# Reordering VectorE's work inside an attention step, and redistributing a small table over other steps

## The chip, the core and the metric

The kernel runs on one core of one Trainium2 chip. The metric is the device time of one execution in microseconds (us), as the median of several runs. Beside it there is one profiled execution, taken by the hardware profiler. Its times stand in the views that this document reads. The engines are called as in the profile: PE is TensorE (PEld its weight loads), DVE is VectorE, ACT is ScalarE, POOL is GpSimd and SP is SyncE. L488 means line 488 of the kernel before.

## What is computed

The input is 32 sequences of 256 tokens with 128 features, in float32. The reference, cut to what matters here:

```python
h = layernorm(x) * (1 + ca) + sa                       # per sequence scale and shift
n = h * rsqrt(mean(h * h) + eps)
q, k, v = n @ W_qkv.T + b_qkv                          # 16 heads of 64
scores = where(causal_mask, -inf, einsum('bqhd,bkhd->bhqk', q, k))
attn = softmax(scores, axis=-2)                        # over the queries
x = x + ga * (attn @ v @ W_o.T + b_o)
h = layernorm(x) * (1 + cb) + sb
x = x + gb * moe(h)      # 32 experts in 4 groups: 2 groups and 6 experts a token,
                         # a shared expert and an anchor expert
```

The softmax runs over the queries of one key. So one partition holds one key's scores, and the sums over the queries scale the values, not the weighted sums.

## The kernel before

**Chunks and steps.** The 8192 tokens are 16 chunks of 512 tokens (2 sequences). Attention runs in steps: step s handles chunk s // 8 and two heads of it, number s % 8. There are 128 such steps and three more that drain. This document calls s % 8 the position of a step, p0 to p7. The expert stage follows after the steps.

**What one step does** (loop at L1098 to L1132). Each engine works through its own queue in the order in which the program was written, so the order of the Python calls is the order on each engine.

- `score_products(s)` (L519, PE): the scores of two sequences times two heads, into four PSUM buffers (pool `ps_sc`, four buffers).
- `lowest(s, b, h)` (L539, DVE): adds the mask, writes the scores into `e` and finds the lowest (the queries were negated, so this is the greatest). It is called four times a step, for sequence b and head h. One call is two pieces of 256 and 128 columns, each with a small read of the accumulator.
- `exponential(s, b, h)` (L549, ACT): four calls a step, each for the `e` of one `lowest`. It also yields the sums.
- `inverse_sums(s - 1)` (L557, DVE) and `scaled_values(s - 1)` (L568, POOL): the values over the sums, as `vs`.
- `weighted_sums(s - 2)` (L586, PE) and `heads_out(s - 2)` (L597, ACT, output `z`).
- `query_product(s + 2)` (L483, PE) and its eviction from PSUM (L488, DVE). `key_product(s + 2)` (L495, PE) and its eviction (L500, ACT).
- `project(s - 3)` (L607, PE) and one quarter of the next values: `values` (L469, PE) and its eviction (L476, DVE).

The query, key and value products share two PSUM buffers (pool `ps_mm`) in turn. So the value product of a step takes the buffer of that step's query product, and waits until the queries are evicted (L488). A product after that takes the buffer of the keys, and waits for their eviction (L500). Two further products use this pool: `route_logits` (L664, at p3) and `route_ranks` (L752 and L756, at p0), each put last in its step.

**Portions.** The rest of the work (the two layer norms and the routing) is cut into portions. A table (L872 to L913) gives each portion a step relative to its chunk, and a place in the step: TOP is ahead of the score products, MID is between the keys' eviction and the projection, END is behind the values. Since eight steps make a chunk, a portion has the same position in every chunk. Those that matter here:

- p0: `route_marks` (L810, DVE, at TOP and MID), `route_ranks` (END). `norm1_scale` (L449 to L452, POOL, END) follows `route_ranks` on POOL.
- p1: `route_weights` (L818 to L828, DVE, TOP), loads of x (END), `rest_bias` (L620, POOL, END).
- p2: `route_place` (L775 to L787, DVE, TOP), `norm1_moments` (L356, DVE, MID), which needs the loaded x.
- p3: `norm2_turn` and `rest_gate` (L652, L628, DVE, TOP), `route_logits` (END).
- p5: `norm1_modulate` (L383, POOL, END). p6: `route_merge` (L692 to L695, DVE, TOP) and `route_groups` (L702 to L715, DVE, MID).
- p7: `route_mask` and `route_top` (DVE), `norm2_modulate` (L383, POOL, END).

**The first tiles' table.** When the routing of chunk 6 is known (step 72), the first tiles of the expert stage can be listed. Nine portions do this with DVE instructions of 4 to 64 elements a partition: `open_first` (L1041), `count_taken` (L1046) and seven steps a to g of `first_tiles.steps()` (L975 to L1034). They depend on each other in this order. Before, they sit at END of steps 80 to 88, one a step (L1084). The table is first read when the expert stage starts, after step 130.

Of the kernel before, what the change touches and what calls it, by code (L numbers as in the profile page):

```python
# [30 lines left out]
NP = H // 2  # L31
# [14 lines left out]
EARLY = 6  # L46
# [10 lines left out]
def adaln_block_kernel(  # L57
# [80 lines left out]
    def late_loads():  # L138

        nc.sync.dma_start(out=wd_sb, in_=w_down.rearrange("(k p) m -> p k m", p=P))  # L140
        nc.sync.dma_start(out=ad_sb, in_=an_down.rearrange("(k p) m -> p k m", p=P))
        nc.sync.dma_start(out=sg_sb, in_=sh_gate)
        nc.sync.dma_start(out=su_sb, in_=sh_up)
        for h in range(P // SI):
            nc.sync.dma_start(out=sd_sb[h * SI : (h + 1) * SI], in_=sh_down)
# [68 lines left out]
    def write_blank(i):  # L214
        nc.sync.dma_start(
            out=rows_d[i * CH : (i + 1) * CH].rearrange("(p i) f -> p i f", i=NT), in_=blank
        )
# [98 lines left out]
    NS = NCH * NP  # L316
# [3 lines left out]
    with ExitStack() as actx:  # L320
# [159 lines left out]
        def query_product(s):  # L480
            c, t = divmod(s, NP)
            pq = ps_mm.tile([P, CH], F32, tag="mm", name=f"pq_{s}")
            nc.tensor.matmul(  # L483
                pq, wqkv_sb[:, 0, t * P : (t + 1) * P], chunk[c]["n"], start=True, stop=True
            )
            q = qk.tile([P, CH], F32, tag="q", name=f"q_{s}")
            step_of["q", s] = q
            return lambda: nc.vector.tensor_scalar(  # L488
                q, pq, -1.0, negbq[:, t : t + 1], ALU.mult, ALU.add
            )  # L490
# [13 lines left out]
        def score_products(s):  # L504


            q, k = step_of.pop(("q", s)), step_of.pop(("k", s))
            ps = []
            for b in range(BPC):
                o = b * S  # L510
                pb = [
                    ps_sc.tile([P, 3 * P], F32, tag="sc", name=f"psc_{s}_{b}_{h}")
                    for h in range(2)
                ]
                for kb in range(2):
                    cols = slice(0, 2 * P) if kb == 0 else slice(2 * P, 3 * P)
                    for h in range(2):
                        r = slice(h * DH, (h + 1) * DH)
                        nc.tensor.matmul(  # L519
                            pb[h][:, cols],  # L520
                            k[r, o + kb * P : o + (kb + 1) * P],
                            q[r, o + kb * P : o + S],
                            start=True,
                            stop=True,
                        )
                ps.append(pb)
            step_of["ps", s] = ps
            step_of["e", s] = [[None, None] for _ in range(BPC)]
            step_of["mn", s] = st.tile([P, BPC, 2, 2], F32, tag="mn", name=f"mn_{s}")
            step_of["sm", s] = st.tile([P, BPC, 2, 2], F32, tag="sm", name=f"sm_{s}")  # L530

        def lowest(s, b, h):

            ps, mn = step_of["ps", s][b][h], step_of["mn", s]
            e = sp.tile([P, 3 * P], F32, tag="e", name=f"e_{s}_{b}_{h}")
            step_of["e", s][b][h] = e
            for kb in range(2):
                cols = slice(0, 2 * P) if kb == 0 else slice(2 * P, 3 * P)
                nc.vector.tensor_tensor_reduce(  # L539
                    e[:, cols], ps[:, cols], mask[:, cols], 1.0, 3e38,  # L540
                    ALU.add, ALU.min, mn[:, b, kb, h : h + 1],
                )

        def exponential(s, b, h):

            e, mn, sm = step_of["e", s][b][h], step_of["mn", s], step_of["sm", s]
            for kb in range(2):
                cols = slice(0, 2 * P) if kb == 0 else slice(2 * P, 3 * P)
                nc.scalar.activation(  # L549
                    e[:, cols], e[:, cols], AF.Exp, bias=mn[:, b, kb, h : h + 1], scale=-1.0,  # L550
                    accum_out=sm[:, b, kb, h : h + 1],
                )

        def inverse_sums(s):
            sm = step_of.pop(("sm", s))
            rc = st.tile([P, BPC, 2, 2], F32, tag="rc", name=f"rc_{s}")
            nc.vector.reciprocal(  # L557
                rc.rearrange("p b k h -> p (b k h)"), sm.rearrange("p b k h -> p (b k h)")
            )
            step_of["rc", s] = rc  # L560

        def scaled_values(s):
            c, t = divmod(s, NP)
            vt, rc = step_of["v", s // HALF], step_of.pop(("rc", s))
            vs = vsp.tile([P, BPC * 2, 2, DH], F32, tag="vs", name=f"vs_{s}")
            col = (t % HALF) * P
            for b in range(BPC):
                nc.gpsimd.tensor_tensor(  # L568
                    vs[:, 2 * b : 2 * b + 2],
                    vt[:, 2 * b : 2 * b + 2, col : col + P].rearrange(  # L570
                        "p k (h d) -> p k h d", h=2
                    ),
                    rc[:, b].unsqueeze(3).to_broadcast([P, 2, 2, DH]),
                    ALU.mult,
                )
            step_of["vs", s] = vs

        def weighted_sums(s):
            vs, es = step_of.pop(("vs", s)), step_of.pop(("e", s))
            pav = ps_av.tile([P, CH], F32, tag="av", name=f"pav_{s}")  # L580
            for b in range(BPC):
                o = b * S
                for kb in range(2):
                    for h in range(2):
                        e = es[b][h]
                        nc.tensor.matmul(  # L586
                            pav[h * DH : (h + 1) * DH, o + kb * P : o + S],
                            vs[:, 2 * b + kb, h, :],
                            e[:, 0 : 2 * P] if kb == 0 else e[:, 2 * P : 3 * P],
                            start=kb == 0,  # L590
                            stop=kb == 1,
                        )
            step_of["pav", s] = pav

        def heads_out(s):
            z = zp.tile([P, CH], F32, tag="z", name=f"z_{s}")
            nc.scalar.copy(z, step_of.pop(("pav", s)))  # L597
            step_of["z", s] = z
# [138 lines left out]
        def new_counts(c):  # L737
            counts[c] = rt.tile([P, NT + 1, NG], F32, tag="cnt", name=f"cnt_{c}", bufs=2)
            return counts[c]
# [130 lines left out]
        TOP, MID, END = range(3)  # L870
# [197 lines left out]
        portions = {}  # L1068

        soon = {-6: 0, -5: 0, -4: 0, -3: 0, -2: 1, -1: 1, 0: 2, 1: 2}  # L1070
        for c in range(NCH):
            for at, where, portion in table[0 if c else NORM1 :]:
                if c == 1 and portion is load_x:
                    continue
                if c == 1:
                    at = soon.get(at + NP, at + NP) - NP
                portions.setdefault(c * NP + at, []).append((where, portion, c))

        def deal(s, where):
            for w, portion, c in portions.get(s, []):  # L1080
                if w == where:
                    portion(c)

        for n, portion in enumerate([open_first, count_taken, *first_tiles.steps()]):  # L1084
            portions.setdefault((EARLY + 4) * NP + n, []).append((END, lambda c, p=portion: p(), 0))
        nc.gpsimd.memset(new_counts(0), 0.0)
        nc.gpsimd.tensor_scalar_mul(counts[0][:, 0, :], origin, first)
        for at in range(min(portions), 0):
# [9 lines left out]
        for s in range(NS + LAG + 1):  # L1098
            if s == NP + 1:
                late_loads()  # L1100
            ahead = s + 2 < NS
            deal(s, TOP)
            if s < NS:
                score_products(s)
                for h in range(2):
                    lowest(s, 0, h)
                for h in range(2):
                    exponential(s, 0, h)
            if 1 <= s <= NS:
                inverse_sums(s - 1)  # L1110
                scaled_values(s - 1)
            if LAG <= s < NS + LAG:
                weighted_sums(s - LAG)
                heads_out(s - LAG)
            if s < NS:
                lowest(s, 1, 0)
                exponential(s, 1, 0)
            if ahead:
                query_product(s + 2)()
            if s < NS:  # L1120
                lowest(s, 1, 1)
                exponential(s, 1, 1)
            if ahead:
                key_product(s + 2)()
            deal(s, MID)
            if LAG < s <= NS + LAG:
                project(s - LAG - 1)
            if s // HALF + 1 < 2 * NCH:
                values(s // HALF + 1, s % HALF)()
            deal(s, END)  # L1130
            for i in blanks[s * 3 : s * 3 + 3]:
                write_blank(i)  # L1132
# [364 lines left out]
```

## Time and profile before

| | |
|---|---|
| runs before: median of 3 (lowest to highest) | 1473.55 us (1470.64 to 1475.26) |
| the profiled execution: its own time | 1488.63 us |
| its span, first to last instruction | 1486.9 us |
| mean granted PE clock over the span | 0.98 |
| busy, share of the span: PE, DVE, ACT, POOL | 95%, 69%, 54%, 52% |
| the attention steps | from about 27 us to about 935 us of the span |
| DVE L539 (lowest), 256 and 128 columns | 406 and 285 ns each |
| DVE L488 (queries' eviction) | 750 ns each, 128 of them |
| ACT L500 (keys' eviction) | 669 ns each |
| POOL L383 (modulate) | 732 ns each |

The page of a profile gives the busy time of each engine, the span in 40 slices, and the costliest groups of instructions with the idle time of their engine just before them and what ended it. Behind the page stand further views. The table of windows gives busy times and the granted PE clock of a stretch. The list of waits says who waited for whom. The timeline shows instructions in order of time: start, duration, engine, line, and in brackets the idle time before it and who ended that. An idle engine costs time only where the engine that sets the pace waits for it.

### The profile page before, as it was taken

The page shows a single profiled execution, that of the slowest core. Times are in us where ns is not written, and L with a number is a line of the kernel's source. Part 1 is how long each engine was busy: PE and PEld are TensorE (multiplying, and loading weights), DVE is VectorE, ACT ScalarE, POOL GpSimd, SP SyncE. Part 2 cuts the span into 40 slices and gives each one's busy share as a digit, 9 for nine tenths or more (in the row PEclk, how much of TensorE's full clock was granted, in tenths as well). Part 3 has the DMA queues.
Part 4 walks back from the last instruction along what each step waited for, and adds up shares of the span by engine and source line. Part 5 has one row for each costly group of instructions (what it writes and reads, how often), then busy time and mean ns, then how long its engine had stood idle before and what let it go on. Part 6 is the DMA issues. An engine that isn't in the chain of part 4 may idle for free. (4 is left out here: it accounts for less than half of the span.)

```text
span 1486.9 us, 29744 instructions
## 1 busy us (share of the span) xinstructions
PE 1413.1 (95%) x8559; PEld 901.8 (61%) x8559; DVE 1033.0 (69%) x4277; ACT 803.5 (54%) x2767; POOL 767.4 (52%) x1294
## 2 busy tenths in 40 slices
PE   7999999999999999999999999889999999999994
PEld 3566666666666666666666666456566666666662
DVE  5666768778777677788787677656755656766664
ACT  4777667677676677667666767323233333333331
POOL 3545457567667657567676655634332233344333
PEclk9999999999999999999999999999999999999997
DMA  4873521121121220221211210577767678887872
GB/s 145 287 241 96 201 70 37 48 68 33 54 65 36 55 57 29 67 53 33 70 43 44 54 32 28 144 191 195 185 183 187 173 210 231 240 251 234 254 201 75
DMA packets 183584, 182.26 MB, mean 123 GB/s; under 512 B 81520, under 2 KB 142656, under 8 KB 178944
## 3 DMA queue, kind: packets, MB, share of 16 engines
q1 hardware_dynamic: 172112, 159.62, 38.8%
q0 software_dynamic: 10624, 20.21, 4.1%
q8 instruction: 71, 1.16, 0.3%
q14 instruction: 89, 0.73, 0.2%
q10 hardware_dynamic: 688, 0.53, 0.1%
HBM read 121.37 MB, written 59.70 MB: 122 GB/s over the span
## 5 line engine op out<-in xcount | busy, mean ns | idle before, releaser
L549 ACT ACTIVATE e<-e,mn 128x256 f32<-128x256 f32 (+1 forms) x1024 | 453.8, 445 | 235.2 <-DVE mn L539 224.8
L539 DVE CUSTOM_DVE_ANT_0 e<-psc,mask 128x256 f32<-128x256 f32 (+1 forms) x1024 | 306.1, 346 | 31.9 <-PE psc L519 28.1
L568 POOL TENSOR_TENSOR vs<-v,rc 128x256 f32<-128x256 f32 x256 | 151.5, 613 | 248.5 <-DVE rc L557 215.9
L1273 POOL DMA_INDIRECT y_d<-y,iy x140 | 137.9, 985 | 235.0 <-ACT y L1270 202.7
L519 PEld LDWEIGHTS psc<-q,k 64*128 64x128 f32 x2048 | 172.7, 194 | 88.7 <-issue 74.3
L1240 DVE TENSOR_TENSOR a<-a,pu 128x512 f32<-128x512 f32 x175 | 120.0, 686 | 148.5 <-PE pu L1237 110.6
L519 PE MATMUL psc<-q,k 64*128 64x256 f32 (+1 forms) x2048 | 211.1, 347 | 0.0
L586 PE MATMUL pav<-e,vs 128*64 128x256 f32 (+1 forms) x2048 | 198.8, 337 | 5.9 <-POOL vs L568 5.9
L1239 ACT ACTIVATE a<-pg 128x512 f32<-128x512 f32 x175 | 104.5, 597 | 183.1 <-PE pg L1236 126.3
L1262 PEld LDWEIGHTS py<-wd_sb,a 128*128 128x128 f32 x1120 | 146.6, 192 | 75.2 <-issue 51.6
L549 ACT ACTIVATION_READ_ACCUMULATOR e<-e,mn 128x1 f32 x1024 | 192.2, 188 | 0.0
L1236 PE MATMUL pg<-h,wg 128*128 128x512 f32 x350 | 181.4, 600 | 0.0
L1237 PE MATMUL pu<-h,wu 128*128 128x512 f32 x350 | 180.1, 596 | 0.0
L607 PEld LDWEIGHTS po<-wo_sb,z 128*128 128x128 f32 x1024 | 135.0, 193 | 59.7 <-issue 56.1
L488 DVE TENSOR_SCALAR q<-pq,negbq 128x512 f32<-128x512 f32 x128 | 96.0, 750 | 103.1 <-PE pq L483 103.0
L586 PEld LDWEIGHTS pav<-e,vs 128*64 128x64 f32 x2048 | 128.9, 139 | 61.1 <-POOL vs L568 6.3
L1262 PE MATMUL py<-wd_sb,a 128*128 x1120 | 148.5, 276 | 5.4 <-DVE a L1241 5.4
L852 POOL DMA_INDIRECT rows_d<-rows,ix x128 | 130.0, 1016 | 37.2 <-issue 34.1
L483 PE MATMUL pq<-n_t,wqkv_sb 128*128 128x512 f32 x256 | 144.9, 648 | 0.7 <-ACT n_t L302 0.7
L476 DVE TENSOR_TENSOR v<-pv,bv_sb 128x512 f32<-128x512 f32 x128 | 88.2, 689 | 75.6 <-PE pv L469 75.5
L607 PE MATMUL po<-wo_sb,z 128*128 128x128 f32 x1024 | 136.3, 277 | 0.0
L469 PE MATMUL pv<-wqkv_sb,n_t 128*128 128x512 f32 x256 | 133.7, 606 | 2.2 <-DVE q L488 1.2
(231 smaller groups left out, 1835.5 us busy)
## 6 DMA issues: line engine op xcount, KB each, us to landing
bt<-cd SPq DMA_DIRECT2D x70, 512.0 KB
rows_d<-blank SPq DMA_DIRECT2D x69, 360.0 KB
rw<-rows_d SPq DMA_DIRECT2D x35, 360.0 KB
wg<-in_w_gate_dram SPq DMA_DIRECT2D x35, 256.0 KB
wu<-in_w_up_dram SPq DMA_DIRECT2D x35, 256.0 KB
bt<-cd SPq DMA_DIRECT2D x140, 64.0 KB
s<-y_d SPq DMA_DIRECT2D x32, 256.0 KB
mb<-mod_dram SPq DMA_DIRECT2D x31, 256.0 KB
```

The lines of the kernel that those rows point to most:

```text
L469: nc.tensor.matmul(pv, chunk[c]["n"][:, i * P : (i + 1) * P], wqkv_sb[:, 2, j * CH : (j + 1) * CH], start=True, stop=True,)
L483: nc.tensor.matmul(pq, wqkv_sb[:, 0, t * P : (t + 1) * P], chunk[c]["n"], start=True, stop=True)
L519: nc.tensor.matmul(pb[h][:, cols], k[r, o + kb * P : o + (kb + 1) * P], q[r, o + kb * P : o + S], start=True, stop=True,)
L539: nc.vector.tensor_tensor_reduce(e[:, cols], ps[:, cols], mask[:, cols], 1.0, 3e38, ALU.add, ALU.min, mn[:, b, kb, h : h + 1],)
L549: nc.scalar.activation(e[:, cols], e[:, cols], AF.Exp, bias=mn[:, b, kb, h : h + 1], scale=-1.0, accum_out=sm[:, b, kb, h : h + 1],)
L568: nc.gpsimd.tensor_tensor(vs[:, 2 * b : 2 * b + 2], vt[:, 2 * b : 2 * b + 2, col : col + P].rearrange("p k (h d) -> p k h d", h=2), rc[:, ...
L586: nc.tensor.matmul(pav[h * DH : (h + 1) * DH, o + kb * P : o + S], vs[:, 2 * b + kb, h, :], e[:, 0 : 2 * P] if kb == 0 else e[:, 2 * P : 3 ...
L607: nc.tensor.matmul(chunk[c]["po"][:, i, :], z[:, i * P : (i + 1) * P], wo_sb[:, t, :], start=t == 0 and i == 0, stop=t == NP - 1 and i == ...
L1236: nc.tensor.matmul(pg, t["wg"][:, k, :], t["h"], start=True, stop=True)
L1237: nc.tensor.matmul(pu, t["wu"][:, k, :], t["h"], start=True, stop=True)
L1262: nc.tensor.matmul(t["py"][:, i, :], a[:, i * P : (i + 1) * P], w, start=k == 0 and i == 0, stop=k == KU and i == NT - 1,)
L1273: sent = nc.gpsimd.indirect_dma_start(out=y_d[:, :], out_offset=bass.IndirectOffsetOnAxis(ap=ix[:, i : i + 1], axis=0), in_=y[:, i, :], in ...
```

## The change

There are two edits in the main loop and its portions.

First, in every step both remaining `lowest` calls (sequence 1, heads 0 and 1) and their exponentials are written ahead of the query product and its eviction. Before, the second of them stood between the queries' eviction and the key product.

Second, the nine portions of the first tiles' table keep their order and place (END), but move from steps 80 to 88 to steps 73, 79, 81, 87, 89, 95, 97, 103 and 105, which are positions p1 and p7 in turn.

```diff
         for n, portion in enumerate([open_first, count_taken, *first_tiles.steps()]):
-            portions.setdefault((EARLY + 4) * NP + n, []).append((END, lambda c, p=portion: p(), 0))
+            at = (EARLY + 3 + n // 2) * NP + (1, 7)[n % 2]
+            portions.setdefault(at, []).append((END, lambda c, p=portion: p(), 0))
...
             if s < NS:
-                lowest(s, 1, 0)
-                exponential(s, 1, 0)
+                for h in range(2):
+                    lowest(s, 1, h)
+                    exponential(s, 1, h)
             if ahead:
                 query_product(s + 2)()
-            if s < NS:
-                lowest(s, 1, 1)
-                exponential(s, 1, 1)
-            if ahead:
                 key_product(s + 2)()
             deal(s, MID)
```

Of each pair of calls such as `query_product(s + 2)()`, the first issues the product on PE and the second the eviction. In the two built programs the queues of PE, ACT, POOL and SP hold the same instructions in the same order. Only DVE's queue differs: the second `lowest` of sequence 1 (four instructions) now stands ahead of L488 instead of behind it, and the table's instructions stand elsewhere.

## The prediction

> **What bounds the kernel now.** I read the busy shares first, then a table of windows, the list of waits inside the attention steps, and the timeline of single steps. Views of before:
>
> ```profile
> PE 1413.1 (95%) x8559; PEld 901.8 (61%) x8559; DVE 1033.0 (69%) x4277; ACT 803.5 (54%) x2767; POOL 767.4 (52%) x1294
> ```
> ```profile
> 43.00:150.00 107.00, 107.00 (x742) 68.12 (x742) 66.40 (x335) 80.58 (x309) 50.33 (x90) 1.00 0.62 209
> ```
> ```profile
> 382.69:439.25 56.56, 54.93 (x382) 35.50 (x381) 43.56 (x230) 39.53 (x154) 37.67 (x69) 1.00 0.20 52
> 439.25:497.36 58.11, 56.56 (x383) 36.60 (x381) 43.70 (x232) 39.63 (x154) 37.93 (x69) 0.97 0.19 50
> ```
> ```profile
> PE pl L664 <- ACT k L500: 13.0, 12, 1.5
> PE pr L752 <- ACT k L500: 4.7, 13, 1.6
> PE pv L469 <- DVE q L488: 1.2, 3, 0.5
> ```
>
> PE sets the pace: from 43 to 150 us it is busy throughout. Between starts of L483 an undisturbed step takes 6.62 us (456.40 to 463.02 in the timeline). Later a chunk takes 55.4 to 60.7 us instead of 8 x 6.62 = 53.0. Read from L483 to L483, p1, p2, p4, p5 and p7 still take 6.62. The rest lies in three places. p0 takes 7.47: the rank product waits about 0.26 for the keys' eviction. p3 takes 8.17 to 11.05: the logits wait 0.46 to 1.52 for the keys, and in some steps the granted clock falls (0.70 from 444.19 to 449.80). p6 takes 6.94 to 7.03: values wait for the queries' eviction. Only a change at these three places, or a new wait, moves the end.
>
> **Edit 1, reordered DVE work.** Nothing is added or removed. The queues of PE, ACT, POOL and SP stay as they are: ACT already did all exponentials ahead of the keys. On DVE the last `lowest` call (from 465.86 to the next start at 466.41: 0.55) moves ahead of L488.
>
> ```profile
> 465.20 0.74 DVE L488 TENSOR_SCALAR q<-pq,negbq 128x512 f32<-128x512 f32 x1
> 465.86 0.41 DVE L539 CUSTOM_DVE_ANT_0 e<-psc,mask 128x256 f32<-128x256 f32 x1
> 466.00 1.12 PE L469 MATMUL pv<-wqkv_sb,n_t 128*128 128x512 f32 x2
> ...
> 466.41 0.17 DVE L702 TENSOR_TENSOR gs<-hi,lo 128x16 f32<-128x16 f32 x1
> ```
>
> *p6, loss.* This is step 62. L488 follows the earlier `lowest` with no idle time and ends at 465.94; the values start 0.06 later. Put behind 0.55 more of DVE work, L488 ends at 466.49 and PE starts at 466.55. Behind this PE work stands the whole next step, with no slack. Eleven steps look so (30, 38, ..., 110): 11 x 0.55 = **+6.05**. Step 22 gives about +0.2 (it has 0.4 of room).
>
> ```profile
> 419.70 0.75 DVE L488 TENSOR_SCALAR q<-pq,negbq 128x512 f32<-128x512 f32 x1 [0.92 <-PE pq L483]
> ...
> 420.82 0.51 ACT L549 ACTIVATE e<-e,mn 128x256 f32<-128x256 f32 x1 [0.18 <-DVE mn L539]
> 421.71 0.67 ACT L500 ACTIVATE k<-pk,bqk_sb 128x512 f32<-128x512 f32 x1
> ...
> 422.52 0.37 PE L752 MATMUL pr<-cnt,ones 128*128 128x20 f32 x2 [0.25 <-ACT k L500]
> ```
>
> *p0, gain.* Here L488 waits 0.92 for its product, and the last `lowest` waits behind it though its scores are ready. It now runs in that idle time. ACT loses its 0.18 of idle and 0.09 of refill, the keys come 0.27 earlier, and the 0.25 wait goes; PE itself is late next. Nine p0 steps are free of the table's portions (24 to 72, 112, 120): 9 x 0.26 = **-2.3**.
>
> *p3, nothing.* In step 59 ACT runs without a gap from 439.47 to the keys' end at 444.13; the last `lowest` (441.40) is not what it waits for. L488 later by 0.55 makes the values wait (0.15 in step 59, up to 0.6 in step 75), but the logits behind them wait for the keys anyway, 1.20: the wait is split, not longer. If that cover were gone it would cost up to 0.6 a chunk, 8 in all.
>
> *Elsewhere, nothing.* At p1, p2, p4, p5 and p7 L488 waits 0.3 to 2.5 for its product, which hides the moved 0.55 wholly or down to 0.1 to 0.2. PE needs L488 only some 0.74 after it ends now. Steps 0 and 1 lose 0.55 each, in front of a 1.62 wait of PE for POOL's `vs` in step 2, where POOL has been busy without a break since 34.0.
>
> **Edit 2, the table.** Its 34 DVE instructions stay; only their place counts. What a portion takes now, from its first start to the start of the next work: `open_first` 0.66, `count_taken` 1.41, a 0.82, b 0.22, c 0.19, d 0.67, e 0.34, f 2.25, g 0.19. f is long because of POOL:
>
> ```profile
> 649.04 0.76 DVE L1016 TENSOR_TENSOR ft_past<-tile_no,ft 128x11 f32<-128x11 f32 x1
> 649.04 1.41 POOL L383 TENSOR_TENSOR rows<-ln_xh,mb 128x256 f32<-128x256 f32 x2
> ...
> 649.72 0.76 DVE L1020 TENSOR_SCALAR ft_blank<-tile_no 128x11 f32<-128x11 f32 x1
> ...
> 650.72 0.17 DVE L1024 TENSOR_TENSOR ft_where<-ft_where,ft_blank 128x11 f32<-128x11 f32 x1
> ```
>
> Instructions of 11 elements take 0.76 while POOL's L383 runs, each ending with one of POOL's, and 0.17 after it. At p7 POOL has about 1.8 us of L383 left when the values' eviction ends. A page of the Trainium skill, "SBUF — State Buffer", section "Who interferes with whom", says that VectorE and GpSimd lock a shared port pair for a whole instruction and the loser blocks. By it a DVE instruction waits for one of POOL's, at most 0.73 by our row. L692 in step 62 took 2.12, through three of POOL's, so the row is worse than the rule. With L692's row instead of f's the sum below would be some 0.2 higher.
>
> So p1 is light, but p7 is not, and its END lies just ahead of p0, where ACT's chain to the keys has no slack. In p0 whatever DVE is late, the rank product waits.
>
> - p7: `count_taken` (step 79) between 1.41 (nothing blocked) and 3.1 (blocked until POOL is done). I take 2.85: 1.9 for the three first instructions, as in f, and six of 0.16. b (87): between 0.22 and 1.9; I take 1.16, two blocked. d (95) 0.67 and f (103) 2.25, as today.
> - p1: these go ahead of p2's `lowest`; there L488 then has 0.6 of room. `open_first` costs 0.2, a 0.3 (with 0.1 of refill on PE), the others nothing.
>
> Today's cost of f is read from step 88: 11.01 instead of 7.47, +3.54, of which 1.54 is fallen clock (its score products took 2.93 instead of 1.58, its weighted sums 1.71 instead of 1.52). A p0 without insertion will be 7.20. New p0 steps: step 80: 7.20 + 2.85 + 1.54 = 11.6 (+4.1). Step 88: 7.20 + 1.16 + half of a clock drop = 9.1 (-1.9). Step 96: 7.87 (+0.4). Step 104: 11.0 (+3.5). After such a late p0 the loads of x are early against PE and the next p3 is short (8.17 in step 91): step 83 9.19 to 8.2 (-1.0), step 107 10.73 to 8.2 (-2.5), step 91 half of the way from 8.17 to 9.99, the mean of the p3 steps 27 to 75, 99 and 107 (+0.9). Steps 82 and 86 lose today's portions (-0.35, -0.39), 74 and 82 gain 0.5. Sum: 4.1 - 1.9 + 0.4 + 3.5 - 1.0 - 2.5 + 0.9 - 0.7 + 0.5 = **+3.3**.
>
> **The sum.** 6.05 + 0.2 - 2.3 + 3.3 = +7.25. The span goes from 1486.9 to 1494.2, the profiled execution from 1488.63 to 1495.9. The runs' median lies 15.1 below that execution; I keep this distance: 1473.55 + 7.25 = **1480.8**. Nothing after step 130 changes except that it starts later.
>
> **Rivals.**
>
> - *Milder table.* At p7 POOL's work and the portions miss each other. With `count_taken` 1.41, b 0.22, d 0.35 and f 0.9, p0 costs +1.1, -3.6, +0.1 and +0.6 in steps 80, 88, 96 and 104, and step 91 goes back to 9.99 (+1.8), with -0.3 from the other steps: -0.3, in all +3.7 or 1477.2. Against it: f and `norm2_modulate` meet at p7 today.
> - *The clock stays up: faster.* The place is p3. With equal waits of 1.32, step 27 took 10.64 and step 51 took 9.03: a drop costs 1.6, and seven p3 steps have one. Today the waits with a drop are 1.08 and longer; 0.95 in step 99 had none. Edit 1 takes 0.03 to 0.6 off the logits' wait and puts it ahead of the values. If a single gap decides, from about 1.07 on, all seven drops go (-11.3), and the two in p0 of the table might (-3): 1480.8 - 14.3 = 1466.5. Against it: step 51 (1.32) and step 83 (1.48) had no drop, so it is not one gap's length alone, and the sum of the idle time stays. The Trainium skill, "TensorE: Matmul & The Clock Gate", Part 1, says that the clock falls after about 3.4 us of idle, by a window that runs freely. By that rule no such wait would drop it; the trace shows drops after 1.1, so the length is wrong here, while a free window fits steps 27 and 51, and by that this rival is worth nothing.
> - *p6 drops the clock: slower still.* The waits of 0.66 that arise there would each cost 1.6 more: 11 x 1.6 = 17.6, 1498. Against it: 0.69 in step 43 had no drop.
>
> **Chances and range.** Forecast (1478 to 1487) 0.60, milder table (1474 to 1479) 0.20, clock up 0.10, p6 drop 0.10. Bounds of the unknown insertions move the forecast by -3 to +3, drops that fall otherwise by as much. The range that leaves out the two outer rivals for the most part is 1471 to 1492. A measurement of this kernel tells about 0.3% (4.4 us) from no change. Slower by more: 0.58 + 0.10 + 0.06 of the milder table = 0.74. Within: 0.02 + 0.14 + 0.03 of the clock = 0.19. Faster: 0.07.
>
> **What will show it.** p6 steps of about 7.55 with values waiting about 0.66 for L488 (right), or 7.0 (wrong). p0 steps of 7.20 with no wait for the keys. `count_taken` in step 79 with 0.7 us instructions, and step 80 above 10. Unchanged p3 waits in sum. Wrong would be my idea of the clock if p3 loses its drops, and my port reading if step 80 is under 9.

## The result, and the profile after

| | before | after |
|---|---|---|
| median of runs (lowest to highest), 14 each on one chip | 1477.57 us (1470.64 to 1487.10) | 1479.22 us (1476.40 to 1486.89) |
| ratio of the times, 95% interval | | 1.0016 [0.9993, 1.0039] |
| profiled execution: its own time, span | 1488.63, 1486.9 us | 1478.40, 1476.6 us |
| mean granted PE clock | 0.980 | 0.985 |

By the ratio the change costs 2.4 us (-1.0 to +5.8), and the interval holds no change. The forecast was 7.25 more, which lies above that interval. The time itself lies inside the range that was given, and the change inside the 0.3% that a measurement can't tell from nothing.

The two profiled executions can't be set against each other as they stand, since after's is the *shorter* one by 10.3 us. As much as that arises behind the attention steps (from 927 us on: 559.9 before, 549.6 after), where the change touches nothing. The steps 0 to 19 went from 135.0 to 137.5, most of it in step 19, where values wait 1.74. The steps 20 to 123 went from 745.6 to 743.0. So the reading goes by steps, from one start of L483 to the next.

The page of after, first line of busy times: PE is as much the pace-setter as before.

```profile
PE 1402.3 (95%) x8559; PEld 896.3 (61%) x8559; DVE 1039.8 (70%) x4277; ACT 797.1 (54%) x2767; POOL 764.3 (52%) x1294
```

The list of PE's waits between 155 and 900 us of after (us in total, times, longest):

```profile
PE pv L469 <- DVE q L488: 12.9, 18, 1.7
PE pl L664 <- ACT k L500: 10.1, 12, 1.0
PE pr L752 <- ACT k L500: 4.0, 4, 1.1
```

Values that wait for the queries' eviction were 3 waits with 1.2 us in sum, and are 18 with 12.9. The rank product waited 13 times and waits 4 times. The logits' waits fell from 13.0 to 10.1, and their longest from 1.5 to 1.0. That last number turns out to be the one that matters most.

**p6 (step 62).** The timeline of after: start, duration, instruction, idle time before it.

```profile
463.83 0.29 DVE L539 CUSTOM_DVE_ANT_0 e<-psc,mask 128x128 f32<-128x128 f32 x1
...
464.05 0.75 DVE L488 TENSOR_SCALAR q<-pq,negbq 128x512 f32<-128x512 f32 x1
...
464.85 1.12 PE L469 MATMUL pv<-wqkv_sb,n_t 128*128 128x512 f32 x2 [0.81 <-DVE q L488]
```

L488 follows the last `lowest` without idle time, and the values wait 0.81 for it. The step took 6.99 and takes 7.70.

**p0 (step 56).** After:

```profile
419.56 0.75 DVE L488 TENSOR_SCALAR q<-pq,negbq 128x512 f32<-128x512 f32 x1 [0.36 <-PE pq L483]
...
421.28 0.67 ACT L500 ACTIVATE k<-pk,bqk_sb 128x512 f32<-128x512 f32 x1
...
422.10 0.37 PE L752 MATMUL pr<-cnt,ones 128*128 128x20 f32 x2
```

L488 still waits for its own product (0.36 instead of 0.92), and the rank product carries no idle time any more. The step went from 7.47 to 7.18.

**p3 (step 59).** The logits of before, then the values and the logits of after:

```profile
444.19 1.08 PE L664 MATMUL pl<-gw_sb,h 128*128 128x32 f32 x8 [1.20 <-ACT k L500]
```
```profile
441.85 1.12 PE L469 MATMUL pv<-wqkv_sb,n_t 128*128 128x512 f32 x2 [0.15 <-DVE q L488]
...
443.94 0.52 PE L664 MATMUL pl<-gw_sb,h 128*128 128x32 f32 x3 [0.96 <-ACT k L500]
```

The wait of 1.20 has become 0.15 ahead of the values and 0.96 ahead of the logits. It is split and hardly shorter. Yet the step took 10.53 and takes 9.09, since the clock stays up.

**The table (steps 79 and 80).** The first instructions of `count_taken` in after, beside POOL's `modulate`:

```profile
586.74 1.40 POOL L383 TENSOR_TENSOR rows<-ln_xh,mb 128x256 f32<-128x256 f32 x2
586.86 0.63 DVE L949 COPY tk<-full 128x4 f32<-128x4 f32 x1
...
587.59 0.57 DVE L954 TENSOR_TENSOR tk<-tk 128x3 f32<-128x3 f32 x1
```

Two instructions of 3 and 4 elements take 0.6 each, and each ends with one of POOL's. The portion lasts from 586.86 to 589.14, 2.28 us, and step 80 is 9.47, which is 7.18 + 2.28.

Where the time of the steps went, us:

| | before | after | change |
|---|---|---|---|
| p6, each of the steps 30 to 110 (step 86 with a portion of the table: 7.38 before) | 6.94 to 7.03 | 7.67 to 7.70 | +0.70 x 11 = +7.7 |
| p0 without the table, nine steps | 7.47 | 7.18 | -0.29 x 9 = -2.6 |
| steps 80, 88, 96, 104 | 7.47, 11.01, 7.47, 7.47 | 9.47, 8.45, 8.00, 10.53 | +3.0 |
| p3, steps 27 to 123 in sum | 123.57 | 112.65 | -10.9 |
| p3 steps 27 to 107 with a fallen clock | 6 of 11 | 0 of 11 | |

### The profile page after: what moved, and what is told of

Read it like the earlier page. It is cut to its first block, busy times and chain, and to the rows that moved or that the text cites. A ratio compares the mean times of both kernels' runs of the same rounds, so it can differ in the third digit from the quotient of the medians.

```text
span 1476.6 us, 29737 instructions
## 1 busy us (share of the span) xinstructions
PE 1402.3 (95%) x8559; PEld 896.3 (61%) x8559; DVE 1039.8 (70%) x4277; ACT 797.1 (54%) x2767; POOL 764.3 (52%) x1294
## 5 line engine op out<-in xcount | busy, mean ns | idle before, releaser
L539 DVE CUSTOM_DVE_ANT_0 e<-psc,mask 128x256 f32<-128x256 f32 (+1 forms) x1024 | 296.8, 345 | 27.0 <-PE psc L519 26.6
L519 PEld LDWEIGHTS psc<-q,k 64*128 64x128 f32 x2048 | 167.8, 188 | 87.5 <-issue 74.3
L519 PE MATMUL psc<-q,k 64*128 64x256 f32 (+1 forms) x2048 | 204.4, 339 | 0.0
L483 PE MATMUL pq<-n_t,wqkv_sb 128*128 128x512 f32 x256 | 144.9, 648 | 0.7 <-ACT n_t L302 0.7
L495 PE MATMUL pk<-n_t,wqkv_sb 128*128 128x512 f32 x256 | 131.7, 596 | 0.0
```

The source lines that it names most:

```text
L483: nc.tensor.matmul(pq, wqkv_sb[:, 0, t * P : (t + 1) * P], chunk[c]["n"], start=True, stop=True)
L519: nc.tensor.matmul(pb[h][:, cols], k[r, o + kb * P : o + (kb + 1) * P], q[r, o + kb * P : o + S], start=True, stop=True,)
L539: nc.vector.tensor_tensor_reduce(e[:, cols], ps[:, cols], mask[:, cols], 1.0, 3e38, ALU.add, ALU.min, mn[:, b, kb, h : h + 1],)
```

## Why p3 became shorter: the clock

The view by windows gives the granted clock of any stretch. Its changes lie on a grid of 3.41 us: in every profile of this study each stretch at lower clock begins a whole number of 3.413 us after the one before it. Three neighbouring cells of before around step 59 (us; PE, PEld, DVE, ACT, POOL busy; PEclk; DMA share; GB/s):

```profile
442.15:445.56 3.41, 2.21 (x14) 1.32 (x15) 1.49 (x5) 2.24 (x10) 2.74 (x3) 1.00 0.16 54
445.56:448.97 3.41, 3.41 (x24) 2.56 (x22) 1.92 (x13) 1.88 (x9) 1.92 (x3) 0.50 0.16 54
448.97:452.38 3.41, 3.41 (x24) 2.13 (x21) 1.44 (x7) 1.78 (x6) 2.92 (x6) 1.00 0.08 27
```

In the first cell PE is idle for 1.20 us (busy 2.21). In the next the clock is half, for exactly one cell. Then it is whole. So a drop is one cell at 0.50, which costs half of 3.41, about 1.7, and 1.6 by the step lengths. Of the 42 drops between 155 and 900 us in the 14 profiles, 39 lasted one cell and three lasted two (step 19 of after and of e3, step 75 of e2). Counted from the first instruction, the grid begins elsewhere in each profile, from 0.21 us (e6) to 3.09 us (d2). The prediction's "0.70 from 444.19 to 449.80" was a mean over cells with and without it.

Over the 14 profiles of this study, from 155 to 900 us, some 2900 cells at full clock had less than 0.95 us of PE idle time in them: after none of these did the clock fall. Single waits of 0.90 to 1.07 had a drop behind them in 10 of 70 cases. For waits of 1.07 and more it depends on where in the cell they begin: in the first 1.3 us, 28 of 29 dropped the clock; later in the cell, 3 of 20. So a wait's length counts, and its place in a free-running grid as well. The bounds 0.95, 1.07 and 1.3 were read off these same waits and not tried on others. Before, the waits were 1.08 to 1.52 in eight of the p3 steps 27 to 107. After, the longest in these eleven is 0.97.

## The experiments

Ratios are against the kernel before, measured beside each run on the same chip, with 95% intervals. "Drops" counts the p3 steps 27 to 107 (eleven) with a fallen clock in the one profiled execution. Times of p6 leave out step 86 where a portion of the table stands there.

**Each edit alone.** `e1_order_only`: edit 1 with the table in its old steps.

```diff
+                for h in range(2):
+                    lowest(s, 1, h)
+                    exponential(s, 1, h)
```

> Edit 1 alone; the table stays in steps 80 to 88. Theory A (gap length): the change costs in structure (p6 11 x 0.70 = +7.7, p0 12 x -0.29 = -3.5), and the split wait of p3 keeps each gap under 1.0 us, so that the p3 steps 27 to 107 have no fallen clock: p3 of 8.2 to 9.2 in the profile, mean granted clock of the runs above that of the runs before, and since both nearly balance a time within 3 us of before. Theory B (chance): the drops of p3 fall by the phase of a free window whatever the order is; then about half of these p3 steps still show score products of 2.4 us or more, the clock of the runs is that of before, and the time is 4.2 us above before.

Measured: 1.0010 [0.9993, 1.0027], 1473.38 us against 1471.42. p6 7.70, p0 7.18 in all steps without the table, step 88 8.91 (11.01 before), 2 drops (83, 107).

`e2_table_only`: edit 2 with the old order in the step.

```diff
+            at = (EARLY + 3 + n // 2) * NP + (1, 7)[n % 2]
+            portions.setdefault(at, []).append((END, lambda c, p=portion: p(), 0))
```

> Edit 2 alone; the order inside a step is the old one. Theory A: p3 waits stay single and 1.1 to 1.5 long, so half or more of the p3 steps keep a fallen clock (10.4 or more), clock as in the runs before, time 2 to 4 us above before by the table (step 80 near 9.5, step 88 near 8.7, step 104 near 10.5). Theory B: the same table cost; drops in p3 by chance, so also as before. Only if p3 had no drops here would the table's new places be what keeps the clock up.

Measured: 0.9998 [0.9977, 1.0018]. Steps 80, 88, 96, 104: 11.43 (with a drop), 8.31, 7.84, 9.17, against 7.47, 11.01, 7.47, 7.47. 3 drops (35, 75, 107).

What follows: neither edit alone can be told from no change. Edit 1's certain costs and gains (+7.7 at p6, and with the table in its old steps -0.29 at eleven or twelve p0 steps, -3.2 to -3.5) would make +4.2 to +4.5, 1.0029 to 1.0031, which lies just outside its interval. So something gives time back with edit 1. Step 88 is 2.1 shorter in this profile, as it has no drop there; p3 is to be looked at for the rest.

**The order at single positions.** `e3_not_p6`: the changed kernel, with the old order at p6. `e4_p0_only`: the old kernel, with the new order at p0. Both by one condition:

```diff
+            early = s % NP != 6        # e3; in e4: s % NP == 0
             if s < NS:
                 lowest(s, 1, 0)
                 exponential(s, 1, 0)
+                if early:
+                    lowest(s, 1, 1)
+                    exponential(s, 1, 1)
             if ahead:
                 query_product(s + 2)()
-            if s < NS:
+            if s < NS and not early:
```

> The changed kernel, but in p6 steps the last lowest stays behind the queries' eviction as before. p6 goes from 7.69 back to 6.99: 11 x 0.70 = 7.7 us less than the changed kernel, about 1471.5 beside 1479.2. Theory A: p3 (new order) has no fallen clock. Theory B: drops in about half of the p3 steps, and then little is gained over before.

Measured: 0.9993 [0.9970, 1.0017], 1469.52. p6 7.13 in the median, not the 6.99 that was expected: some of the loss at p6 is made elsewhere. Drops 51 and 91.

> The old kernel, but in p0 steps the last lowest goes ahead of the queries' eviction. The p0 steps go from 7.47 to 7.18 (12 of them: -3.5 us), p6 stays at 6.99. Theory A: p3 keeps its old order, its single waits of 1.1 to 1.5 and its drops, so the time is 3 to 4 us under before and the clock as before. Theory B: the same -3.5, with drops by chance.

Measured: 0.9985 [0.9967, 1.0002]. p0 7.18 in every step without the table, p6 6.94 to 7.09, p3 unchanged with 5 drops. The gain at p0 is what the forecast said, and it is made at p0 alone.

`e8_not_p4_p6`: the new order except at p4 and p6, the table in its old steps.

```diff
+            early = s % NP not in (4, 6)
```

> The new order in all steps but p4 and p6; table in its old steps. The run without p6 still had p6 at 7.13 instead of 6.94 to 7.0. Theory A for that rest: at p4 the new order moves the sum at L635 by 0.55 into POOL's power (L350, 1.34 instead of 1.04), POOL is late from there to its L383 at p5, and DVE's merge at p6 is blocked that much longer; then p6 falls to 6.94 to 7.0 here. Rival: it comes from p5's own new order, and p6 stays at 7.13. Time some 7 to 9 us under before, as p0 and p3 have the new order.

Measured: 0.9955 [0.9934, 0.9976], 1465.23. p6 is back at 6.94, and no drop in 27 to 107. So p4 is the place of the rest. In the timeline of after at p4 (step 60), DVE's L635 (the sum into x) starts 0.24 ahead of POOL's L350 and runs beside it. L680 and L684 are DVE's next work for the routing (`route_pairs`):

```profile
449.88 0.68 DVE L635 TENSOR_TENSOR x<-xt,o_t 128x512 f32<-128x512 f32 x1
450.12 1.34 POOL L350 TENSOR_TENSOR ln_out<-ln_in,mhalf 128x4 f32<-128x4 f32 x1
...
452.36 0.41 DVE L680 TENSOR_TENSOR scb<-sig,gb_sb 128x128 f32<-128x128 f32 x1
452.80 0.36 DVE L684 TENSOR_TENSOR hi<-scb 128x64 f32<-128x64 f32 x1
```

The same work in step 44 of before, where POOL is as far in its work as in after:

```profile
337.37 1.04 POOL L350 TENSOR_TENSOR ln_out<-ln_in,mhalf 128x4 f32<-128x4 f32 x1
...
337.67 0.68 DVE L635 TENSOR_TENSOR x<-xt,o_t 128x512 f32<-128x512 f32 x1
...
339.61 0.28 DVE L680 TENSOR_TENSOR scb<-sig,gb_sb 128x128 f32<-128x128 f32 x1
339.92 0.27 DVE L684 TENSOR_TENSOR hi<-scb 128x64 f32<-128x64 f32 x1
```

L350 takes 1.34 where L635 has started ahead of it, and 1.04 where L635 starts 0.30 behind it, though the two run beside each other there too. So what counts is which of them starts first. POOL's next work (L373) then comes 0.3 later. DVE's L680 and L684 run beside it in both kernels, but now take 0.41 and 0.36 instead of 0.28 and 0.27, and DVE is some 0.2 late. At p5 `inverse_sums` (L557) is 0.21 later, counted from the start of the step, and POOL's `vs` and L383 behind it are 0.21 and 0.22 later. The delay reaches them through DVE: POOL itself stands idle for 0.70 ahead of `vs` in both kernels. At p6 L383 holds L692 and L693 on DVE 0.2 longer, which puts L488 later. This chain is read from the timelines; that p4's order causes the 0.19 is shown by e3 (7.13) and e8 (6.94).

**The gain at p3.** `e5_p0_p3`: the old kernel, with the new order at p0 and p3 only.

```diff
+            early = s % NP in (0, 3)
```

> The old kernel, with the new order in p0 and p3 steps only; table in its old steps. Theory A (an idle gap of PE above about 1.0 us may drop the clock, and the new order at p3 holds the logits' wait at 0.97): p0 7.18, p6 6.94 to 7.0, and of the eleven p3 steps 27 to 107 about one has a fallen clock instead of four or five: 3.5 us less from p0 and about 6 less from p3, some 9 under before. Theory B (drops by chance): 3.5 less, and four or five p3 steps of 10.4 or more in the profile.

Measured: 0.9972 [0.9945, 0.9998], 1466.15. p3's longest waits are 0.96 and 0.97; 2 drops (27, 35), both behind a wait of 0.96 to 0.97.

Taken together, p3 steps 27 to 107 with x loaded late had 15 drops in 44 in the old order (before, e2, e4 and e9 below) and 6 in 55 in the new order (after, e1, e3, e5, e8). That is most of the gain: a longest wait that is held under 1 us. The idle time itself falls little, from 12.4 to 10.6 in the mean of these profiles.

One profile for each kernel is a small sample, and the profile of before is an extreme one: its mean granted clock is 0.980, where the runs of before in the experiments have 0.985. But the mean granted clock of all runs says the same:

| | new order at p3: e1 | e3 | e5 | e8 | old order: e2 | e4 | e9 |
|---|---|---|---|---|---|---|---|
| runs of before | 0.9851 | 0.9851 | 0.9847 | 0.9847 | 0.9851 | 0.9851 | 0.9850 |
| runs of the experiment | 0.9879 | 0.9872 | 0.9868 | 0.9876 | 0.9842 | 0.9837 | 0.9862 |

One drop takes 0.5 x 3.41 us out of some 1470, 0.0012 of the mean. By this estimate the new order at p3 takes 1.8 to 2.5 drops off a run, 3 to 4 us. In the old order a run has 1.1 drops fewer to 1.2 more, which is no more than such means leave open (1.2 to 1.8 each). The times alone don't show it at p3: e5 is 4.1 below before, of which p0 accounts for 3.5 (12 x 0.29).

Why the wait is held under 1 us is seen in step 59. In the new order the values wait for L488, which stands behind the last `lowest`, and the keys come behind that `lowest`'s exponentials. Both are tied to one point, so wherever the values of these steps wait for L488 (0.07 to 0.50), the logits wait 0.96 or 0.97. What more there is of lateness stands ahead of the values.

`e6_x_early`: the old kernel, with x loaded two steps earlier. The late DVE work at p3 begins with `norm1_moments` at p2, which waits for x.

```diff
-            (-15, END, load_x),
+            (-17, END, load_x),
```

> The old kernel, with the loads of x two steps earlier, so that the moments at p2 need not wait for them. The logits' wait at p3 falls from 0.7 to 1.5 to about 0.46 in every chunk, as in steps 115 and 123 today. Theory A: no p3 step from 27 to 107 has a fallen clock and each takes 8.17: -0.65 x 11 for the waits and about -7 for the drops, some 14 us under before. Theory B: drops still come in about four of the eleven, and only some 7 us are gained.

Measured: 0.9915 [0.9886, 0.9944], 1458.50. All p3 steps take 8.16 to 8.17 with a wait of 0.46 and no drop, except 83 (10.72, after the table). So most of p3's wait beyond 0.46 came from the load of x.

**The clock's condition.** Three probes take the early load, where all p3 waits are equal, and lengthen one wait by needless work: copies on ACT ahead of the last exponentials, in d3 also fills on DVE ahead of L488. Their extra work is part of their time, and each has one run.

```diff
+            if (s + LAG) % NP == 3 and s + LAG > 18:
+                for r in range(3):                # d1; 6 in d2 and d3
+                    nc.scalar.copy(extra_a, z[:, 0:P])
```

> A probe of the clock on the old kernel with early loads of x (logits' wait 0.46 at p3 in every chunk, no drops). At p3 ACT makes three extra copies of 128 columns behind z, which nothing reads, so that the keys come some 0.7 later and PE waits once, about 1.1 to 1.2, ahead of the logits in steps 19 to 107 and later. Theory A (the length of one gap): a fallen clock in about half of these p3 steps, as with waits of 1.0 to 1.2 so far. Theory of the sum (all idle time of PE within some 3 us counts): the same.

Measured: span 1485.3. The wait is 1.45 in thirteen p3 steps (19 to 123 without 83). Ten of them take 10.73 to 10.79 with a fallen clock, and three (43, 75, 107) take 9.15 to 9.16 without: a drop costs 1.63. In e6, which lacks only the copies, the same steps waited 0.46 and had none. The view by windows of d1, the cell of the wait and the cell behind it, first in step 59, then in step 75:

```profile
445.59:449.00 3.41, 1.96 (x14) 1.32 (x14) 1.31 (x2) 2.24 (x10) 2.70 (x3) 1.00 0.25 81
449.00:452.41 3.41, 3.41 (x24) 2.55 (x22) 1.92 (x13) 1.87 (x9) 1.19 (x3) 0.50 0.08 27
561.64:565.05 3.41, 1.96 (x13) 1.13 (x11) 1.70 (x8) 2.74 (x11) 2.54 (x3) 1.00 0.14 54
565.05:568.46 3.41, 3.41 (x38) 2.70 (x37) 1.82 (x13) 1.85 (x8) 1.54 (x2) 1.00 0.16 54
```

The two cells hold the same idle time (3.41 - 1.96 = 1.45). Behind the first the clock is 0.50, behind the second 1.00. What differs is the wait's place. Counted from the start of its cell, it begins at:

| step | 19 | 27 | 35 | 43 | 51 | 59 | 67 | 75 | 91 | 99 | 107 | 115 |
|---|---|---|---|---|---|---|---|---|---|---|---|---|
| wait begins at, us | 0.79 | 0.77 | 1.24 | 1.55 | 0.22 | 0.58 | 0.92 | 1.37 | 0.58 | 0.90 | 1.35 | 0.02 |
| drop | yes | yes | yes | no | yes | yes | yes | no | yes | yes | no | yes |

A chunk with a drop lasts 58.0 to 58.5, close to 17 cells (58.03), so the place moves on by 0 to 0.5 from one chunk to the next until it passes about 1.3. Then one chunk goes without a drop and is shorter. This also answers why drops came in rows before: they start at 445.56, 503.58 and 561.61 there, 58.02 and 58.03 apart, 17 cells. A kernel with a period near 17 cells meets the grid at the same place again and again.

> The same probe with six extra copies: one wait of about 1.8 to 2.0 ahead of the logits at p3. Theory A: a fallen clock in nearly all p3 steps. Theory of the sum: the same.

Measured: span 1458.7, all p3 steps 8.49, no drop. The probe didn't make the wait that it was to make. The timeline of d2 in step 59 (its lines 501 and 668 are L500 and L664):

```profile
435.47 1.08 PE L668 MATMUL pl<-gw_sb,h 128*128 128x32 f32 x8 [0.78 <-DVE v L477]
...
436.41 0.67 ACT L501 ACTIVATE k<-pk,bqk_sb 128x512 f32<-128x512 f32 x1
```

The logits run before the keys' eviction begins, and wait for the values' eviction instead. So with six copies they seem to have the other of the pool's two buffers; the profile leaves buffer numbers out, and why the built program deals so is not shown. So d2 says nothing of waits of 2 us. It shows only that waits of 0.78, one in each of fourteen p3 steps, drop no clock, and that the logits' wait for the keys can give way to another wait.

> The same six extra copies on ACT, so that the keys come as late as in the probe before, and five fills by DVE of a tile that nothing reads ahead of the queries' eviction at p3, so that part of PE's wait moves ahead of the values: about 0.6 to 1.0 there and the rest ahead of the logits, with the same sum. Theory A: clearly fewer fallen clocks than in the probe before, few if both parts are under 1.0. Theory of the sum: as many as there.

Measured: span 1459.2, p3 again 8.49 (step 83: 9.41) with the logits waiting 0.78 for the values' eviction. The probe missed for the same reason; only step 83 had two waits (0.66 and 0.78, no drop). Whether two waits in one cell count as their sum was left without a clean test. Over all profiles, fourteen cells held two waits and 1.07 or more of idle time in sum: six had a drop behind them, eight (sums up to 1.52, the longer part inside the cell 0.80 to 1.05) had none. It stays open.

**Other places for the table, and all together.** `e9_table_p3`: the old kernel, with the portions at END of p3 and p1 steps.

```diff
+            at = (75, 83, 91, 97, 99, 107, 113, 115, 121)[n]
```

> The old kernel with the table's portions at p3 and p1 steps (75, 83, 91, 97, 99, 107, 113, 115, 121) and nothing else changed. Where DVE idles behind the portion the table costs nothing: no p0 step above 7.47, so step 88 goes from 11.01 to 7.47, steps 82 and 86 back to 6.62 and 7.0. Some 4 us under before, less what the later p3 of that chunk gives back (step 91 from 8.17 to about 9.5): 2 to 4 under. Rival (the table costs wherever it is): no difference.

Measured: 0.9995 [0.9972, 1.0018]. Every p0 step takes 7.47, step 88 too, so the table is out of the way there. In this profile the p3 waits of 1.01 to 1.28 begin 1.25 to 3.19 into their cells and none dropped the clock; the one of 1.40 (step 59) begins at 1.04 and did. The runs spread from 1459.5 to 1475.4, so the 3.5 us that step 88 gave back can't be seen in the median. For the table's worth alone this is inconclusive.

`e7_all`: the new order at p0 and p3, x two steps earlier, the table as in e9.

> What the experiments point to, together: new order in p0 and p3 only, loads of x two steps earlier, and the table's portions at p3 and p1 steps (75, 83, 91, 97, 99, 107, 113, 115, 121), where DVE idles behind them (p3) or they are short (p1). Theory A: p0 7.18 everywhere, p3 8.17 to 8.2, p6 6.94 to 7.0, no step 80 to 104 above 7.2 but p3: 3.5 + 14 + 4 = about 20 us under before. Theory B: about 13 under before, with drops left in p3.

Measured: **0.9863 [0.9834, 0.9892]**, 1450.82 us (1448.83 to 1452.97) against 1472.09. PE's waits between 155 and 900 us of e7:

```profile
PE pl L664 <- ACT k L500: 6.5, 14, 0.5
PE pav L586 <- ACT e L549: 2.0, 1, 2.0
PE pv L469 <- DVE q L488: 0.2, 1, 0.2
```

p0 takes 7.18, p3 8.16 to 8.17, p6 6.93 to 7.07, in every chunk. The steps 20 to 123 take 719.8 (745.6 before). The runs spread over 4 us, those of before beside them over 13. Its interval lies below that of after (0.9993 to 1.0039).

## Why the prediction was right and where it was wrong

The forecast was a loss of 7.25, above the interval of what was measured (-1.0 to +5.8). The prediction gave 0.74 to a loss clear of the 0.3% and 0.19 to what came, a change inside it. That 1479.22 lies 1.6 from the forecast 1480.8 is luck: the kernel before took 1477.57 in these runs, 4.0 more than the 1473.55 from which the sum starts. In the sum p6 was put too small, the table too large, and a gain at p3 was left out; the errors partly cancel.

- **p6, right in place and cause, too small in size (0.55 for 0.70).** "Put behind 0.55 more of DVE work" came true for L488 itself. Measured were +0.70 a step, +7.7 for +6.05. The other 0.15 comes from p4 (e3, e8), where DVE's L635 now starts ahead of POOL's L350. The prediction counted L488's place in each step alone ("elsewhere, nothing") and missed that 0.55 of reordering at p4 changes which instructions of DVE and POOL hold each other up.
- **p0, right.** 7.20 forecast, 7.18 measured, no wait for the keys, 9 x 0.29 (e4 shows it alone).
- **The table, at p0 half of what was forecast.** Forecast for steps 80, 88, 96, 104: 11.6, 9.1, 7.87, 11.0; measured: 9.47, 8.45, 8.00, 10.53. `count_taken` took 2.28 for 2.85: two blocked instructions, not three. The clock drop of 1.54 that was put on step 80 didn't come (its longest wait is 1.06); in e2 it did, with 11.43. Steps 83, 91, 107 came out at 8.31, 9.23, 8.17 (forecast 8.2, 9.1, 8.2). Sum of the four p0 steps: +6.1 forecast, +3.0 measured. Step 91's +0.9 and the -3.5 of steps 83 and 107 aren't the table's alone, since p3 changed as a whole. Steps 74 and 82 gave +0.17 and +0.30 (forecast +0.5 and +0.15).
- **p3, the step that failed.** "The wait is split, not longer" is right: the waits of the steps 27 to 107 sum to 12.5 before and 10.3 after. What failed is the inference that an unchanged sum costs the same. It stands in the prediction twice: "p3, nothing", and the rival dismissed with "a free window fits steps 27 and 51, and by that this rival is worth nothing". The window is free, and it still needs a single wait of about 1.07 or more in most cases. Splitting 1.08 to 1.52 into 0.96 and a rest takes most drops away: 6 of 11 p3 steps had one before and 0 of 11 after, 15 of 44 and 6 of 55 over all profiles with the late load. By the prediction's own sign ("if p3 loses its drops") its idea of the clock was wrong.
- **The rival "the clock stays up" was half right.** Its place and its price (1.6 a drop) are as measured. Its size was not: it took seven drops a run as certain. A run's drops depend on the grid, which lies elsewhere in each profile. As an estimate, +2.4 measured, less 7.7 at p6, plus 2.6 at p0, less 3.0 for the table, leaves -5.7 (3.4 either way) for p3 and all else that differs, where the two profiles show -10.9 at p3 and the rival asked for -14.3. The granted clocks above put the drops that go at about two a run.
- **"p6 drops the clock"** fell: eleven waits of 0.78 to 0.81 without a drop, and no cell at full clock with less than 0.95 of idle time had one behind it in any profile here.

The Trainium skill, "TensorE: Matmul & The Clock Gate", Part 1, says that the window is free-running, 3413 ns long, and that the clock is either whole or half. The runs agree: cells of 3.41, 1.00 or 0.50. It also says that the clock goes down after at least one idle window, and warns of idle gaps over about 3.4 us. There the measurement decides: waits of 1.08 to 1.74 dropped it, 28 times of 29 where they began in the cell's first 1.3 us.

Open: what exactly brings the clock down, since d1's steps 43, 75 and 107 hold 1.45 of idle time wholly inside a cell and had no drop; and whether two waits in a cell add up.

## What to carry to other kernels

Where PE sets the pace, look for its longest single wait in each stage, not for the sum: here waits under 0.95 us cost their own length, and waits of 1.07 and more cost 1.6 us more in 31 of 49 cases. Work that is moved past an eviction is priced at every position of the period where that eviction has no slack (p6), and also by which instructions of DVE and POOL it makes meet a step later. Apply such a reordering only at the positions that gain, and first remove the late load that makes the wait (e6 gave 0.85% with one number).

## What the runs showed that was not expected

- The clock falls to 0.50 for one cell of 3.41 us (in three of 42 cases for two) behind a wait of little over 1 us; the grid is the same through a whole execution, and a period of 17 cells (58.03 us) keeps meeting it at the same place.
- A POOL power over 4 elements (L350) took 1.34 us instead of 1.04 where a two-input DVE instruction (L635) had started 0.24 ahead of it. Where L635 started 0.30 behind it, neither took longer (1.04 and 0.68). So POOL can be held up by DVE as well, and the order of their starts decides it here.
- What a product waits for can change when another engine's work grows: with six copies on ACT the logits waited 0.78 for the values' eviction (d2, d3), with three 1.45 for the keys' (d1).
